# One ordered region from the first stream to the end, with layer 1's first entry laid into turns 10 to 13 of the hyperbolic stage

## The chip, the cores and the metric

The kernel runs on one core of one Trainium2 chip. The metric is the device time of one execution in microseconds (us). Before the change it is 3591.77 us, the median of 3 runs (3590.89 to 3592.56). The core's engines have instruction queues of their own and meet only at semaphores: PE multiplies matrices and transposes tiles, DVE, ACT and POOL work element by element, and SP issues most DMAs.

## The reference

A decoder of two layers works on `x` of 4 sequences of 512 rows and 256 columns, with a context of 4 sequences of 1024 rows and 128 columns. Each block adds to `x`:

```python
x = x + L0_attn(layernorm(x))        # landmark attention
x = x + L0_xattn(layernorm(x), ctx)  # causal attention and attention to the context
x = x + L0_ffn(layernorm(x))         # a linear layer with 6-bit quantisation
x = x + L1_attn(layernorm(x))        # hyperbolic attention, 16 heads of 16
x = x + L1_xattn(layernorm(x), ctx)  # double cross-attention, 16 heads of 32
x = x + L1_ffn(layernorm(x))         # 8 experts, the best 2 of them
```

Two of these matter here. The hyperbolic attention lifts queries and keys onto a hyperboloid, and its scores are the negative squared distances:

```python
neg_inner = einsum('bhie,bhje->bhij', tq, tk) - einsum('bhid,bhjd->bhij', sq, sk)
dist = arccosh(maximum(neg_inner, 1.0 + 1e-07))
scores = -dist ** 2 / sqrt(D)        # then causal mask, softmax, times the spike mask
y = einsum('bhij,bhjd->bhid', attn, v)
```

The double cross-attention, called with an already normalised input, begins with two more norms, the second of them inside its first attention:

```python
x = _ln(xx, ln1_g, ln1_b)            # xx = layernorm(x): a norm of a norm, then scale and shift
xn = _ln(x, lnx_g, lnx_b)            # yn is normed in the same way with lny_g, lny_b
```

## The kernel before, in words

**Stages.** The program runs layer 0's attention, layer 0's cross-attention (a `Stream`, L590 and on, which lays the work of many small attention jobs into steps), layer 1's hyperbolic attention (`l1_attn`, called the hyperbolic stage below), layer 1's cross-attention (`l1_xattn`, another `Stream`) and the experts. Layer 0's quantised linear layer and the lift to the hyperboloid are made in chains of small pieces, one chain for each batch; those that the first stream does not get done are handed on to the hyperbolic stage in a list called `left`.

**Regions.** Inside `with tc.manual_schedule()` instructions keep the order in which the program issues them. Before the change there are three such regions: the first stream's `s.run()`, the loop over the hyperbolic turns, and the second stream's `s.run()` with what follows. What lies outside, and where one region stands against another, is placed by a scheduler. In the built program of before, the first pieces of the second stream stand on DVE's, POOL's and SP's lists in the midst of the hyperbolic turns.

**The hyperbolic stage.** It has 16 units: 4 batches, 2 halves of the heads (`hh`), and 2 pairs of query tiles, (3, 0) and (2, 1). Each pair has 640 columns of causal scores, in 4 tiles `s` (and 4 `mh`) of 128 x 2 x 640. The loop overlaps three units: turn i, in program order on all engines, does

1. for every second turn `fetch`: the DMA of the next `qk` (and `v`) on SP;
2. `squares` of unit i-1: 4 multiplications on POOL (L1047);
3. `roots` of unit i: for each of the 4 tiles two square roots on ACT (L1030, L1031) and an add on POOL (L1032), then two small roots (L1035, L1036) and a small add on POOL (L1037) for the row minima `lm`; then one `pump()`;
4. `scores` of unit i+1: matmuls on PE (L1015, L1019) and clamps on DVE (L1020), which also give the minima;
5. `finish` of unit i-2: transposes, reciprocal and products on DVE; for `hh` = 1 also the projection and the add to `x`;
6. `outputs` of unit i-1: 16 exponentials on ACT (L1066), 10 groups of transposes on PE (L1072), each with a copy on DVE (L1074) and then matmuls (L1059), with a `pump()` after each pair of `gg` and query tile (after copies 4, 5, 9, 10 for the pair (3, 0); 3, 5, 8, 10 for (2, 1));
7. `logs` of unit i: a small logarithm on ACT (L1040), a small square on POOL (L1041), and 4 logarithms on ACT (L1043), which the squares of the next turn need.

The pool of `s` has 9 tiles and that of `mh` has 6. So the second and third roots of turn i need the first five transposes of unit i-2 to be read, and the second half of the scores of unit i+1 waits for POOL's first two adds L1032 of unit i.

**pump.** `left` is a list of chains; each of their items has a gap, counted in calls of `pump`, and a function that issues instructions. One call issues the items of the first chain that are due. Before the change `fetch(b, hh)` pumps until no more than B - 1 - b chains are left, and for the last batch it calls `done()`, which frees the first stream's memory on the right and builds `Early`: the loads of the second stream's first constants and weights (`bc5`, `pv5`, `wk`, `wv`, `wq`).

**The entry.** For each batch of the second stream's first attention, the entry is: a copy of `x` to DRAM (`kept`, DMA on SP); a norm applied twice over (`ln_pieces` with `twice`): two halves of the statistics on DVE (L153 to L159), a power on POOL (L164), `again` (5 small DVE instructions and a second L164), and `apply` in two halves (small DVE instructions L169 to L172 and two L192 each); `enter`, a scale and a shift on POOL (L1141, L1142); and a second norm with one power. In before, `block(k, b)` (L1221 and on) makes all of them and puts them into the second stream's chain.

Of the kernel before, what the change touches and what calls it, by code (L numbers as in the profile page):

```python
# [12 lines left out]
F32 = mybir.dt.float32  # L13
# [7 lines left out]
P = 128  # L21
B, T, C = 4, 512, 256
TC, CC = 1024, 128
NT = T // P
# [13 lines left out]
def decoder_kernel(ctx: ExitStack, tc: tile.TileContext, a: dict, out: bass.AP):  # L38
    nc = tc.nc
    V, G, S, PE = nc.vector, nc.gpsimd, nc.scalar, nc.tensor  # L40

    def ts(i, n=P):
        return slice(i * n, (i + 1) * n)
# [12 lines left out]
    zpool = pool(ctx, "z", 2)  # L56
# [29 lines left out]
    x = const.tile([P, NTILE, C], F32, name="x", tag="x")  # L86
# [430 lines left out]
    def l0_xattn(w, wc, wp, bq, bc2, ct_d, front):  # L517
        with ExitStack() as st:
# [160 lines left out]
            for b in range(B):  # L679
                batch(b)  # L680
            s.chain([(8 + i, 16 + 2 * i, gap, c, f) for i, (gap, c, f) in enumerate(front.weights())])
            with tc.manual_schedule():
                return s.run()

# [252 lines left out]
    def l1_attn(wo, spk, qk_d, v_d, left, done):  # L937
        with ExitStack() as st:
# [27 lines left out]
            units = []  # L966
# [11 lines left out]
            def pump():  # L978
                pump.n += 1
                if left:  # L980
                    c = left[0]
                    while c.items and pump.n >= c.at + c.items[0][2]:
                        c.at = pump.n
                        c.items.popleft()[4]()
                    if not c.items:
                        left.pop(0)
# [3 lines left out]
                c.at = -99  # L990

            def fetch(b, hh):
                while len(left) > B - 1 - b:
                    pump()
                if (b, hh) == (B - 1, 0):
                    done()
                if hh == 0:
                    vs[b] = vp.tile([P, NT, VW], F32, name="v", tag="v")
                    nc.sync.dma_start(vs[b], v_d[b])
                qks[b, hh] = qp.tile([P, 2, 2, T], F32, name="qk", tag="qk")  # L1000
                nc.sync.dma_start(qks[b, hh], qk_d[b][:, :, ts(hh, 2), :])


            def scores(u):
# [21 lines left out]
            def roots(u):  # L1026
                u.s = []
                for m in u.m:
                    s = sp_.tile([P, 2, 640], F32, name="s", tag="s")
                    S.activation(s, m, AF.Sqrt, bias=bpos, scale=2.0**-20)  # L1030
                    S.activation(m, m, AF.Sqrt, bias=bneg, scale=2.0**-20)  # L1031
                    G.tensor_add(s, s, m)  # L1032
                    u.s.append(s)
                u.lm = wk.tile([P, 2, 8], F32, name="lm", tag="lm")
                S.activation(u.lm, u.mn, AF.Sqrt, bias=bpos, scale=2.0**-20)  # L1035
                S.activation(u.mn, u.mn, AF.Sqrt, bias=bneg, scale=2.0**-20)  # L1036
                G.tensor_add(u.lm, u.lm, u.mn)  # L1037

            def logs(u):
                S.activation(u.lm, u.lm, AF.Ln, scale=1024.0)  # L1040
                G.tensor_mul(u.lm, u.lm, u.lm)  # L1041
                for s in u.s:
                    S.activation(s, s, AF.Ln, scale=1024.0)  # L1043

            def squares(u):
                for s in u.s:
                    G.tensor_mul(s, s, s)  # L1047
# [61 lines left out]
                        PE.matmul(ps[:, 0:C], yT[:, c, :], wo[:, c, :], start=c == 0, stop=c == 1)  # L1109
                    add_to(x[:, u.b * NT + qt, :], ps[:, 0:C])  # L1110

            with tc.manual_schedule():
                fetch(0, 0)
                n = len(units)
                prev_o = None
                for i in range(-1, n + 2):
                    u = units[i] if 0 <= i < n else None
                    p = units[i - 1] if 0 <= i - 1 < n else None
                    nx = units[i + 1] if 0 <= i + 1 < n else None
                    if nx and nx.qts[0] == 2 and i >= 0:  # L1120
                        k = 2 * nx.b + nx.hh + 1
                        if k < 2 * B:
                            fetch(k // 2, k % 2)
                    if p:
                        squares(p)
                    if u:
                        roots(u)
                        pump()
                    if nx:
                        scores(nx)  # L1130
                    if prev_o:
                        finish(*prev_o)
                        prev_o = None
                    if p:
                        prev_o = (p, outputs(p))
                    if u:
                        logs(u)


    def affine(dst, src, g, b):  # L1140
        G.tensor_mul(dst, src, mid_bc(g, NT))  # L1141
        G.tensor_add(dst, dst, mid_bc(b, NT))  # L1142


    class Early:
        def __init__(self):
            self.stack = ExitStack()
            self.pl = pool(self.stack, "l5e", 1, "right")
            self.bc5 = load_bc(self.pl, "bc5", 2048)
            self.pv5 = load(self.pl, "pv5", a["pv5"], [P, 44])  # L1150
            self.inner = self.stack.enter_context(ExitStack())
            self.att = pool(self.inner, "l5b", 1, "right")
            self.w = {}
            self.attn_weights("a1", 2, self.w)

        def attn_weights(self, p, nk, w):
            w["k"] = load(self.att, "wk5", rows(f"{p}_wk"), [P, nk, 512])
# [4 lines left out]
    def l1_xattn(cn_d, moe, early):  # L1162
        with early.stack as st:
# [12 lines left out]
            dram = st.enter_context(tc.tile_pool(name="l5x", bufs=1, space=bass.MemoryType.DRAM))  # L1176
            bc5, pv5 = early.bc5, early.pv5
            kept = [dram.tile([P, NT, C], F32, name=f"kept{b}", tag=f"kept{b}") for b in range(B)]
# [42 lines left out]
            def block(k, b):  # L1221
# [5 lines left out]
                e = SimpleNamespace()  # L1227

                def z():
                    if not hasattr(e, "z"):  # L1230
                        e.z = zpool.tile([P, NT, C], F32, name="ln_z", tag="ln_z")
                    return e.z

                def z3():
                    if not hasattr(e, "z3"):
# [2 lines left out]

                def arrive():
                    assert not k or b in back  # L1240

                def enter():
                    affine(x1, e.z, bc5[:, ts(2 * k, C)], bc5[:, ts(2 * k + 1, C)])

                def begin():
                    e.xnT = wk.tile([P, 2, T], F32, name="xnT", tag="xnT")
# [131 lines left out]

                f0, a0 = jobs[k, b, 0].first_d, jobs[k, b, 0].first_a
                own = []  # L1380
                if k == 0:
                    own.append((f0 - 20, f0 - 18, 1, 0.0, lambda: nc.sync.dma_start(kept[b], x1)))
                first, second = ln_pieces(x1, z, twice=k == 0), ln_pieces(x1, z)

                fr = f0 - (12 if k and b == 0 else 20)
                own.append((fr, max(fr, f0 - 17), 0, 0.0, arrive))
# [31 lines left out]
            for k in range(2):  # L1418
                for b in range(B):
                    block(k, b)  # L1420
            with tc.manual_schedule():
                s.run()
                slots.end()

# [382 lines left out]
    with ExitStack() as mid:  # L1807
        mp = pool(mid, "mid", 1)
        dram = mid.enter_context(tc.tile_pool(name="l4d", bufs=1, space=bass.MemoryType.DRAM))
        spk = mp.tile([P, B, NT], F32, name="spk", tag="spk")  # L1810
        qk_d = [dram.tile([P, 2, 4, T], F32, name=f"qk_d{b}", tag=f"qk_d{b}") for b in range(B)]
        v_d = [dram.tile([P, NT, VW], F32, name=f"v_d{b}", tag=f"v_d{b}") for b in range(B)]
        bc3 = load_bc(mp, "bc3", C)
        wqkv = load(mp, "w4", rows("l1_wqkv"), [P, 2, 769], eng=nc.scalar)
        bc4 = load_bc(mp, "bc4", 1026)
        right = mid.enter_context(ExitStack())
        front = Front(right, bc3, wqkv, bc4, spk, qk_d, v_d)
        with ExitStack() as early:
            wp = pool(early, "early", 1)
            first = ExitStack()  # L1820
            fp = pool(first, "first", 1)
            w1 = load(fp, "w1", rows("l0_w"), [P, 2, 768])
            bc1 = load_bc(fp, "bc1", 768)
            w = {n: load(wp, f"w2{n}", rows(f"l0x_{n}"), [P, 2, 512], eng=nc.scalar) for n in ("q", "k", "cq")}
            w["v"] = load(wp, "w2v", rows("l0x_v"), [P, 2, C], eng=nc.scalar)
            wc = {n: load(wp, f"w2{n}", rows(f"l0x_{n}"), [P, 1, m], eng=nc.scalar) for n, m in (("ck", 512), ("cv", C))}
            wo0 = load(wp, "w2p", rows("l0x_p"), [P, 2, C], eng=nc.scalar)
            bq = load(wp, "bq", a["bq"], [P, 16], eng=nc.scalar)
            bc2 = load_bc(wp, "bc2", 768)
            with first as st:  # L1830
                psum_pairs(st)
                l0_attn(w1, bc1)
                context_T(ct_d, cn_d, pvc)
                clear_rows(moe, fp)
            S.preload_act_table_set("natural_log_exp_and_others")
            left = l0_xattn(w, wc, wo0, bq, bc2, ct_d, front)
        mp = pool(mid, "mid2", 1)
        wo1 = load(mp, "w4o", rows("l1_wo"), [P, 2, C])
        early = []

        def done():
            right.close()
            early.append(Early())

        l1_attn(wo1, spk, qk_d, v_d, left, done)
    l1_xattn(cn_d, moe, early[0])

# [83 lines left out]
```

## Time and profile before

| | us |
|---|---|
| median of 3 runs | 3591.77 |
| profiled execution | 3592.31 |
| its span | 3590.6 |
| stretch 0 to 1147: layer 0 | 1147 |
| stretch 1147 to 1710: hyperbolic stage | 563 |
| stretch 1710 to 3200: double cross-attention | 1490 |
| stretch 3200 to 3590: experts | 390 |
| PE, DVE, ACT, POOL busy | 3178.6, 2146.9, 1614.8, 825.2 |

The stretches are cut at round times near the stages' ends. The mean clock that the throttle granted to PE in the profiled execution is 0.918 of full speed. In the stretch from 1540 to 1710 PE is busy for 129.09 of 170.00 us, DVE for 110.22, ACT for 146.67 and POOL for 115.29; from 1710 to 3200 PE is busy for 1418.52 of 1490.

A line of the timeline gives the start in us, the length in us, engine, line of the program, operation, output and inputs with their shapes, how many instructions of a run are put together (x), and in brackets how long the engine had waited before it and for what. L-numbers are lines of the kernel before. In the slices of the page each digit is the busy share of one fortieth of the span, in tenths.

### The profile page before, as it was taken

Reading aid. Unit: us, or ns where it says so; the run is one execution under the profiler, and the core shown is the slowest. Engines: PE = TensorE matmul, PEld = TensorE weight load, DVE = VectorE, ACT = ScalarE, POOL = GpSimd, SP = SyncE. Lnnn points to the kernel's source line nnn. Section 1 sums busy time; section 2 is a strip of 40 time slices with the busy share of each in tenths; the row PEclk is TensorE's granted clock in tenths of the full one; section 3 lists DMA queues with packets and bytes.
Section 4 is the critical chain, followed back from the end, with each engine's and each line's share of the span. In section 5 each row is a group of like instructions: output and inputs, shape, how many; then the busy total and the mean of one; then the engine's idle time right before and its main releaser. Section 6 shows DMA issues by size and latency. Waiting matters only on the chain.

```text
span 3590.6 us, 51432 instructions
## 1 busy us (share of the span) xinstructions
PE 3178.6 (89%) x20119; PEld 1513.5 (42%) x20119; DVE 2146.9 (60%) x5068; ACT 1614.8 (45%) x2860; POOL 825.2 (23%) x763
## 2 busy tenths in 40 slices
PE   6689999999998576687998999999999999989994
PEld 3433333334334343444333344433333333448994
DVE  4576666776775778766666555555646656443112
ACT  2235554454554876697233334334443343433331
POOL 1010112122022845676122121110101111020003
PEclk9789999999998576788899999999999999989997
DMA  8200000000002000300000000000000000035885
GB/s 274 66 14 7 1 7 4 24 10 7 24 1 70 24 1 31 107 13 7 24 1 1 1 1 18 7 1 30 13 1 13 7 1 15 4 110 206 317 328 170
DMA packets 81396, 176.13 MB, mean 49 GB/s; under 512 B 6265, under 2 KB 63745, under 8 KB 76033
## 3 DMA queue, kind: packets, MB, share of 16 engines
q1 hardware_dynamic: 76016, 161.16, 12.7%
q0 software_dynamic: 3072, 8.39, 0.8%
q8 instruction: 158, 2.59, 0.3%
q10 hardware_dynamic: 2064, 3.29, 0.3%
q14 instruction: 86, 0.70, 0.1%
HBM read 127.48 MB, written 45.34 MB: 48 GB/s over the span
## 4 chain that ended last, share of the span: by engine, by line
PE 69%; DVE 16%; ACT 4%; issue 4%; DMA 3%; POOL 2%; SPq 0%; POOLq 0%; ACTq 0%; DVEq 0%
PE ps_s L363 16%; PE ps_g L452 7%; PE ps_s L389 5%; PE ps_g L459 4%; PE ps_s L1742 3%; PE ps_s L1749 3%; PE ps_s L1342 3%; PE ps_s L1282 3%; PE ps_s L588 3%; DVE mx L371 3%; PE ps_s L1327 3%; PE ps_s L382 3%; PE ps_s L1072 2%; PE ps_s L1314 1%; DMA rows<-ln_z,idx 1%
## 5 line engine op out<-in xcount | busy, mean ns | idle before, releaser
L390 ACT ACTIVATE pt<-ps_s 128x512 f32<-128x512 f32 (+2 forms) x1536 | 791.4, 569 | 1033.5 <-PE ps_s L389 895.5
L371 DVE TENSOR_REDUCE mx<-ps_s 128x1 f32<-128x512 f32 x1280 | 818.5, 684 | 415.5 <-PE ps_s L363 307.6
L363 PE MATMUL ps_s<-kT,qT 32*128 32x512 f32 (+3 forms) x3072 | 921.7, 623 | 41.6 <-DVE mx L371 39.5
L389 PE MATMUL ps_s<-qa,kT 32*128 32x512 f32 (+3 forms) x1536 | 446.7, 599 | 3.0 <-DVE mx L371 1.6
L363 PEld LDWEIGHTS ps_s<-kT,qT 32*128 32x128 f32 x3072 | 307.1, 186 | 322.0 <-DVE mx L371 133.7
L389 PE MATMUL ps_s<-qT,kT 32*128 32x512 f32 x1536 | 410.5, 624 | 0.0
L459 PE MATMUL ps_g<-pt,onesf 128*32 128x512 f32 x1536 | 214.0, 629 | 0.0
L1032 POOL TENSOR_TENSOR s<-s,mh 128x1280 f32<-128x1280 f32 x64 | 186.9, 2945 | 68.0 <-ACT mh L1031 49.1
L164 POOL TENSOR_TENSOR ln_r<-ln_ve,mhalf 128x4 f32<-128x4 f32 x40 | 41.1, 1028 | 625.7 <-DVE ln_ve L159 560.9
L1303 POOL TENSOR_TENSOR yT<-o 128x128 f32<-128x128 f32 x128 | 58.1, 457 | 535.1 <-DVE o L1302 532.8
L1744 ACT ACTIVATE hid<-ps_s,we 128x128 f32<-128x128 f32 x312 | 89.0, 370 | 201.4 <-PE ps_s L1742 163.0
L367 DVE CUSTOM_DVE_ANT_0 junk<-ps_s,dmask 128x512 f32<-128x512 f32 (+3 forms) x256 | 125.7, 491 | 88.2 <-PE ps_s L363 44.9
L389 PEld LDWEIGHTS ps_s<-qa,kT 32*128 32x128 f32 x1536 | 148.7, 188 | 52.0 <-DVE mx L371 31.1
L1015 PE MATMUL ps_s<-qk 32*128 32x256 f32 (+3 forms) x512 | 103.1, 609 | 62.9 <-DVE mh L1020 56.6
L382 PE MATMUL ps_s<-qm,all 3*128 3x512 bf16 x768 | 149.3, 387 | 6.5 <-DVE v L1290 4.0
L1742 PE MATMUL ps_s<-zsT,we 128*128 128x128 f32 x1248 | 148.1, 277 | 7.8 <-DVE zsT L1733 7.3
L1742 PEld LDWEIGHTS ps_s<-zsT,we 128*128 128x128 f32 x1248 | 146.4, 194 | 11.8 <-DVE zsT L1733 8.6
L1047 POOL TENSOR_TENSOR s<-s 128x1280 f32<-128x1280 f32 x64 | 147.6, 2339 | 12.3 <-ACT s L1043 12.3
L1072 PE MATMUL ps_s<-ident,s 128*128 128x128 f32 x640 | 129.7, 340 | 18.3 <-ACT s L1066 17.1
L1074 DVE COPY pt<-ps_s 128x512 f32<-128x512 f32 x160 | 108.6, 688 | 56.7 <-PE ps_s L1072 56.5
L1749 PE MATMUL ps_s<-we,hid 128*128 128x256 f32 x624 | 141.0, 379 | 0.0
L452 PE MATMUL ps_g<-pt,vc 128*32 128x512 f32 x1024 | 138.2, 611 | 0.0
(425 smaller groups left out, 4986.7 us busy)
## 6 DMA issues: line engine op xcount, KB each, us to landing
we<-in_we SPq DMA_DIRECT2D x39, 2052.0 KB, 10.0
rows<-zero SPq DMA_DIRECT2D x8, 2048.0 KB, 16.7
qk_d<-qkT SPq DMA_DIRECT2D x32, 256.0 KB, 2.6
qk<-qk_d SPq DMA_DIRECT2D x8, 1024.0 KB, 6.5
zs<-rows SPq DMA_DIRECT2D x39, 128.0 KB, 4.8
outs<-ys SPq DMA_DIRECT2D x39, 128.0 KB, 5.3
li<-in_a_li SPq DMA_DIRECT2D x4, 1024.0 KB, 8.7
v_d<-vp SPq DMA_DIRECT2D x16, 143.5 KB, 1.8
```

The lines of the kernel that those rows point to most:

```text
L363: PE.matmul(ps[:, 0:n], u.qT[r, ts(qt)], u.kT[r, hf * 512 : hf * 512 + n], start=True, stop=True)
L371: V.tensor_reduce(m, ps[:, 0:n], AX.X, ALU.max)
L382: PE.matmul(ps, self.ones[r, :], u.qm[r, :], start=True, stop=False)
L389: PE.matmul(ps[:, c0:], u.kT[r, ts(kt)], (u.qa if u.first_row else u.qT)[r, c0:], start=u.first_row, stop=True)
L390: S.activation(u.pt[:, j, c0:], ps[:, c0:], AF.Exp, scale=u.scale)
L452: PE.matmul(o[r, c0:], u.v(kt, j), pt[:, j, c0:], start=first, stop=last)
L459: PE.matmul(acc[ts(j, 32), 1, :], self.onesf, pt[:, j, :], start=i == 0, stop=i == u.nkt - 1)
L1032: G.tensor_add(s, s, m)
L1047: G.tensor_mul(s, s, s)
L1072: PE.transpose(ps[:, ts(j)], u.s[h // 2][:, h % 2, c0 : c0 + P], ident)
L1742: PE.matmul(ps[:, ts(f)], u.w[:, k : k + P], u.zT[:, c, :], start=c == 0, stop=c == 1)
L1749: PE.matmul(ps[:, 0:C], u.h[:, f, :], u.w[:, 2048 + f * C : 2048 + f * C + C], start=f == 0, stop=f == 7)
```

## The change

Two things are done. First, one region takes the place of the three: it is opened before the first stream's table of activations is loaded and closed at the end of the second stream, so that everything in between keeps the order in which the program issues it. Second, the entry of batch 0 is no longer built by `block(0, 0)`. A new method `Early.entry` makes the pieces of an entry, and `Early.pieces` puts those of the first one, with the copy `kept[0]`, into one chain, which `done()` appends to `left`; so `pump` issues them in the hyperbolic turns. `fetch` pumps only when `hh` is 0, and calls `done()` behind the loads of `v` and `qk`; after the loop the rest of `left` is pumped. The `kept` tiles are made in `Early`.

With the gaps given, the pieces fall so in program order: in turn 10 the copy `kept[0]` (after the roots), the two halves of the statistics (after copies 3 and 5 of the outputs) and `again` (after copy 10); in turn 11 the two halves of `apply` (after copies 4 and 9) and `enter` (after copy 10); in turn 12 the second norm's statistics and its first `apply` half (after copy 10); in turn 13 the second half. PE's and ACT's lists are the same as before. On POOL, the two powers stand between L1037 and L1041 of turn 10, the affine L1141 and L1142 there in turn 11, the power of the second norm there in turn 12. On SP, `v` and `qk` of batch 3 stand before the loads of `bc5`, `pv5`, `wk`, `wv`, `wq`; `kept[0]` after them; then `qk` of batch 3's other half, `li1`, `li2`, `li3` and `kept` of batches 1 to 3.

```diff
@@ l0_xattn
-            with tc.manual_schedule():
-                return s.run()
+            return s.run()
@@ l1_attn
             def fetch(b, hh):
-                while len(left) > B - 1 - b:
+                while hh == 0 and len(left) > B - 1 - b:
                     pump()
-                if (b, hh) == (B - 1, 0):
-                    done()
                 if hh == 0:
                     vs[b] = vp.tile([P, NT, VW], F32, name="v", tag="v")
                     nc.sync.dma_start(vs[b], v_d[b])
                 qks[b, hh] = qp.tile([P, 2, 2, T], F32, name="qk", tag="qk")
                 nc.sync.dma_start(qks[b, hh], qk_d[b][:, :, ts(hh, 2), :])
+                if (b, hh) == (B - 1, 0):
+                    done()
...
-            with tc.manual_schedule():
-                fetch(0, 0)
-                n = len(units)
...
+            fetch(0, 0)
+            n = len(units)
...
+            while left:
+                pump()
@@ class Early, __init__
+            dram = self.stack.enter_context(tc.tile_pool(name="l5x", bufs=1, space=bass.MemoryType.DRAM))
+            self.kept = [dram.tile([P, NT, C], F32, name=f"kept{b}", tag=f"kept{b}") for b in range(B)]
+            self.e = SimpleNamespace()
+
+        def entry(self, k, b, e):
+            x1 = x[:, ts(b, NT), :]
+            def z():
+                if not hasattr(e, "z"):
+                    e.z = zpool.tile([P, NT, C], F32, name="ln_z", tag="ln_z")
+                return e.z
+            def enter():
+                affine(x1, e.z, self.bc5[:, ts(2 * k, C)], self.bc5[:, ts(2 * k + 1, C)])
+            return ln_pieces(x1, z, twice=k == 0), enter, ln_pieces(x1, z)
+
+        def pieces(self):
+            first, enter, second = self.entry(0, 0, self.e)
+            work = [(1, 0.0, lambda: nc.sync.dma_start(self.kept[0], x[:, 0:NT, :]))]
+            work += [(2 if i > 1 else 1, 0.0, p) for i, p in enumerate(first)] + [(1, 0.0, enter)]
+            return work + [(2 if i in (0, 2) else 1, 0.0, p) for i, p in enumerate(second)]
@@ l1_xattn, block(k, b)
+                begun = (k, b) == (0, 0)
+                e = early.e if begun else SimpleNamespace()
...
-                if k == 0:
+                if k == 0 and not begun:
                     own.append((f0 - 20, f0 - 18, 1, 0.0, lambda: nc.sync.dma_start(kept[b], x1)))
-                first, second = ln_pieces(x1, z, twice=k == 0), ln_pieces(x1, z)
+                first, enter, second = ([], lambda: None, []) if begun else early.entry(k, b, e)
...
-            with tc.manual_schedule():
-                s.run()
-                slots.end()
+            s.run()
+            slots.end()
@@ the program
+            ordered = ExitStack()
+            ordered.enter_context(tc.manual_schedule())
             S.preload_act_table_set("natural_log_exp_and_others")
             left = l0_xattn(w, wc, wo0, bq, bc2, ct_d, front)
...
         def done():
             right.close()
             early.append(Early())
+            work = early[0].pieces()
+            left.append(SimpleNamespace(items=deque((0, 0, gap, c, f) for gap, c, f in work), at=-99))
...
     l1_xattn(cn_d, moe, early[0])
+    ordered.close()
```

More of the change, by code (lines that the diff above doesn't have):

```diff
@@ L1110, in finish @@
                     add_to(x[:, u.b * NT + qt, :], ps[:, 0:C])
-            with tc.manual_schedule():
-                fetch(0, 0)
-                n = len(units)
[L1115 to L1137, printed above, removed]
+            fetch(0, 0)
+            n = len(units)
+            prev_o = None
+            for i in range(-1, n + 2):
+                u = units[i] if 0 <= i < n else None
+                p = units[i - 1] if 0 <= i - 1 < n else None
+                nx = units[i + 1] if 0 <= i + 1 < n else None
+                if nx and nx.qts[0] == 2 and i >= 0:
+                    k = 2 * nx.b + nx.hh + 1
+                    if k < 2 * B:
+                        fetch(k // 2, k % 2)
+                if p:
+                    squares(p)
+                if u:
+                    roots(u)
+                    pump()
+                if nx:
+                    scores(nx)
+                if prev_o:
+                    finish(*prev_o)
+                    prev_o = None
+                if p:
+                    prev_o = (p, outputs(p))
+                if u:
+                    logs(u)
+            while left:
+                pump()
     def affine(dst, src, g, b):
@@ L1175, in l1_xattn @@
             ptp = pool(inner, "l5p", 2)
-            dram = st.enter_context(tc.tile_pool(name="l5x", bufs=1, space=bass.MemoryType.DRAM))
             bc5, pv5 = early.bc5, early.pv5
-            kept = [dram.tile([P, NT, C], F32, name=f"kept{b}", tag=f"kept{b}") for b in range(B)]
+            kept = early.kept
             onesf = att.tile([P, 32], F32, name="onesf", tag="onesf")
@@ L1226, in block @@
                 bl1, bl3 = bc5[:, ts(4 + 2 * k, C)], bc5[:, ts(5 + 2 * k, C)]
[L1227 to L1232, printed above, removed]
+                begun = (k, b) == (0, 0)
+                e = early.e if begun else SimpleNamespace()
                 def z3():
@@ L1240, in arrive @@
                     assert not k or b in back
-                def enter():
-                    affine(x1, e.z, bc5[:, ts(2 * k, C)], bc5[:, ts(2 * k + 1, C)])
                 def begin():
```

## The prediction

> **What bounds the kernel now.** First the page's slices (89.8 us each): PE is the full row everywhere except slices 14 to 19, the hyperbolic stage, where ACT rises.
>
> ```profile
> span 3590.6 us, 51432 instructions
> PE   6689999999998576687998999999999999989994
> ACT  2235554454554876697233334334443343433331
> ```
>
> Then the timeline of each engine there. A plain turn (here turn 11):
>
> ```profile
> 1563.22 7.36 ACT L1066 ACTIVATE s<-s,lm 128x512 f32<-128x512 f32 x16
> 1570.48 0.20 ACT L1040 ACTIVATE lm<-lm 128x16 f32<-128x16 f32 x1
> 1576.63 1.36 ACT L1030 ACTIVATE s<-mh,bpos 128x1280 f32<-128x1280 f32 x1
> ...
> 1566.51 0.21 POOL L1037 TENSOR_TENSOR lm<-lm,mn 128x16 f32<-128x16 f32 x1
> 1570.75 0.22 POOL L1041 TENSOR_TENSOR lm<-lm 128x16 f32<-128x16 f32 x1 [4.03 <-ACT lm L1040]
> 1571.91 9.16 POOL L1047 TENSOR_TENSOR s<-s 128x1280 f32<-128x1280 f32 x4 [0.94 <-ACT s L1043]
> 1581.03 11.46 POOL L1032 TENSOR_TENSOR s<-s,mh 128x1280 f32<-128x1280 f32 x4
> ```
>
> Call the start of the exponentials (L1066) in turn i E_i: E9 1495.95, E10 1537.26, E11 1563.22, then 25.96 apart up to E15 1667.06. ACT has no gap in 25.96, so a plain turn is ACT's. POOL works 21 of the 26 and rests only between L1037 and L1041. L1037 ends at E+3.5, and ACT's L1040 needs it at E+7.26: POOL may be 3.8 us late, no more. Next, what happens when something is late:
>
> ```profile
> 1500.59 2.35 POOL L1141 TENSOR_TENSOR x<-ln_z,bc 128x1024 f32<-128x1024 f32 x1 [3.28 <-DMA bc<-in_bc]
> ...
> 1505.40 0.43 DVE L155 BATCH_NORM_STATS2 ln_st<-x 128x6 f32<-128x256 f32 x1 [2.82 <-POOL x L1142]
> 1509.56 2.28 DVE L169 TENSOR_TENSOR ln_t<-ln_r 128x4 f32<-128x4 f32 x1 [1.13 <-POOL ln_r L164]
> 1516.43 2.24 DVE L172 TENSOR_TENSOR ln_r<-ln_r,ln_t 128x4 f32<-128x4 f32 x1
> 1518.70 3.25 DVE L192 TENSOR_SCALAR ln_z<-x,ln_mv,ln_r 128x256 f32<-128x256 f32 x2
> 1522.54 1.27 DVE L1074 COPY pt<-ps_s 128x512 f32<-128x512 f32 x2
> ...
> 1527.35 1.36 ACT L1030 ACTIVATE s<-mh,bpos 128x1280 f32<-128x1280 f32 x1 [15.24 <-DVE pt L1074]
> ```
>
> That is turn 9: the entry of layer 1 holds the copies L1074, and ACT stands 15.24 us. Four single waits complete the picture:
>
> ```profile
> 1351.13 0.22 ACT L1040 ACTIVATE lm<-lm 128x16 f32<-128x16 f32 x1 [9.04 <-POOL lm L1037]
> ...
> 1375.49 0.66 PE L1059 MATMUL ps_g<-pt,v 128*32 128x128 f32 x8 [5.99 <-DVE pt L1074]
> ...
> 1380.68 0.16 DVE L172 TENSOR_TENSOR ln_r<-ln_r,ln_t 128x4 f32<-128x4 f32 x1
> ...
> 1583.96 0.56 DVE L1020 TENSOR_SCALAR_CACHE_REDUCE mh<-ps_s 128x384 f32<-128x384 f32 x1 [1.68 <-POOL s L1032]
> ```
>
> A late POOL stops ACT at L1040; late DVE stops PE; L172 costs 0.16 with POOL idle but 2.24 while POOL runs; and the second half of the scores (L1020) waits for POOL's first two adds L1032.
>
> **What the change removes.** In before the entry's first norm sits in turns 5 and 6, its affine and second norm in turn 9.
>
> Turn 9 without it: the scores end at 1502.33; finish with its projection takes 7.9 (1618.32 to 1626.20 in turn 13), so the copies start at 1510.2 instead of 1522.54. ACT's second root needs the fifth transposes, 4.44 after the first copy (1626.20 to 1630.64): 1514.75 instead of 1527.35. Turn 9 lasts 28.7, not 41.3: −12.65. Ends: −8.0 (only the DMA wait and the two affines) and −15.3 (down to a plain turn).
>
> Turn 6: DVE's entry work between 1359 and 1389 leads to PE's 5.99 above and a smaller one. Without it the second token's L826 starts at 1367.0 (after L842) instead of 1373.04, but its L828 then meets POOL's L1032 (1366.95 to 1369.9), and the fourth token's L828 the add after ACT's late roots. Followed to the output copy at 1389.47, that leaves −4.4. Ends: −1.1 (POOL's power, 1.13, alone) and −9.3 (all of PE's waits there: 5.99, 0.68, 1.60, 1.07).
>
> **What it adds.** PE and ACT keep their order in the built program. POOL's is now: two powers (L164) between L1037 and L1041 of turn 10, the affine (L1141, L1142) there in turn 11, one power there in turn 12. Each waits for DVE pieces that lie inside the outputs, and L1041, the squares L1047 and the adds L1032 queue behind. Unlocked prices: a half of the statistics 1.07, `again` 1.4, `apply` 1.75 and 0.75, a power 1.02, the affine 4.75. Times go on from E10 = 1524.65, leaving turn 6 aside.
>
> Turn 10: the copies start at 1529.8; statistics end at 1535.9; `again` follows the tenth copy (1540.65) and ends at 1542.05; the second power ends at 1543.1. L1047 starts at 1543.4, where a plain turn has E+8.69 = 1533.3: 10.1 late. L1037 of turn 11 ends at 1564.2 (9.1 + 11.5 later), L1040 wanted it at 1557.9. ACT stands 6.35.
>
> Turn 11: the second half of the scores waits for the adds at 1555.4 and 1558.3; finish meets two adds; copies start at 1564.4, `apply` ends at 1575.1, the affine at 1579.9. L1047 1580.15, L1037 of turn 12 at 1600.9. ACT wanted it at 1590.2: 10.7, and two of its roots then wait 2.4 and 1.0 for late transposes.
>
> Turn 12: scores again wait for adds (1592.15, 1595.0), finish meets two more and projects; copies start at 1607.7, the power is done at 1615.5. POOL now catches up without a rest to 1636.5, and `apply` (from 1619.15) meets it: L169 to L172 and L192 take 12.2, as the same ones took 12.3 in turn 9 of before. Then scores to 1642.0, finish with locks, copies at 1651.75.
>
> Turn 13: ACT waits 6.1 at L1040 and 10.85 for the transposes (1656.2). E14 = 1666.1, E15 = 1692.05, and from there ACT leads as before.
>
> So E11 to E12 is 32.35 (+6.4), to E13 40.1 (+14.1), to E14 43.05 (+17.1): +37.6. Lower end: copies always at E+3.1 and no locks: L1047 at least 6.6 late in turn 10 and 10 in turn 11, less 3.8 each: +9. Upper: the second L192 of each pair locked too, twice 2.87: +43.3. I take 37.6, as each link has its row above.
>
> The Trainium skill (SBUF — State Buffer, "Who interferes with whom") says that of a VectorE instruction in a two-port mode, or with two SBUF inputs, and a GpSimd one, the later blocks until the other is through. Rows 2.24 and 0.16 agree. It speaks against laying small VectorE steps beside a busy POOL, and taken for each instruction it would lock both L192 of a pair, the upper end: 3618. The row 3.25 for two shows one lock, but POOL rested after it.
>
> **At nothing.** v and qk of batch 3 now go ahead of bc5 on SP (0.34 + 0.53 us): bc5 is read some 70 us later. The kept copy of batch 0 lands 2.6 us after issue, long before turn 11; without that cover it would hold the affine. li1 moves behind qk: first read at 1889. li3 now stands before the kept copies of batches 1 to 3, waits until 1704 as before, so batch 1's lands near 1707.6; its affine runs at 1732.05. That cover gone, POOL would wait there. The memsets and identb only swap places.
>
> **Sum.** −12.65 − 4.4 + 37.6 = +20.6. The profiled execution took 3592.31 (span 3590.6 and 1.7 around), 0.54 over the median 3591.77 of three runs; on that median: 3612.3.
>
> **Rivals.** Faster: POOL's holds stay inside its 3.8 us, only −17.1 is left: 3574.7. It decides at turn 10's L1047: before 1537 it is hidden. Against it: the power must wait for the tenth copy, E+13 at the soonest. Chance 0.08. Milder: the holds as worked out, but POOL is through when `apply` comes in turn 12, so 10.85 goes: 3601.4; for it speaks that E13 could shift by a few us, against it that POOL is 14 us behind. 0.17. Harsher: both L192 locked, 3618 and up with the next scores late: 0.12. No effect: the two norms cost the same wherever they lie, 3592; against it, 15.24 goes from one wait and returns on POOL: 0.05. The forecast: 0.58.
>
> **Numbers.** A run tells 0.2% (7.2 us) from no change. Faster 0.08, same 0.05 (no effect), slower 0.87 (forecast, milder, harsher). The range 3594 to 3627 leaves out the faster case and the ends of the others.
>
> **What would show it.** Right: turn 9 near 29 us; POOL idle before L164 in turn 10 and before L1141 in turn 11 for DVE; ACT waiting at L1040 for L1037 in three turns, 6 to 11 each; L169 to L172 over 2 us each in turn 12. Wrong: L1040 never waits, or turns 10 to 13 stay at 26.

## The result

The changed kernel takes 3612.81 us, the median of 5 runs (3610.21 to 3614.08); the kernel before takes 3591.77 (5 runs, 3587.57 to 3592.56). The ratio is 1.006, with a 95% interval of 1.0045 to 1.0074: slower by 21 us. The forecast was 3612. The profiled execution took 3611.71 us, 19.4 more than that of before, with a span of 3610.0.

The page's slices of the changed kernel (90.3 us each):

```profile
span 3610.0 us, 51409 instructions
PE   6689999999998576856898999999999999989994
ACT  2235554454554776777233343344344343433331
```

PE's row has a new dip behind the place where the entry was laid (5 and 6 instead of 8 and 7, about 1625 to 1805). Instructions of the hyperbolic stage have line numbers lower by one than before (L1040 is L1039, L1037 is L1036, L1047 is L1046, L1066 is L1065). The time between the first exponentials of successive turns, taken from ACT's timeline, tells turn by turn where the time went (a plain turn is 25.96):

| us | turn 9 | 10 | 11 | 12 | 13 | 14 | 10 to 14 over plain |
|---|---|---|---|---|---|---|---|
| before | 41.31 | 25.96 | 25.96 | 25.96 | 25.96 | 25.96 | 0 |
| changed | 28.33 | 25.96 | 31.81 | 39.11 | 47.69 | 25.96 | 40.7 |

The waits of ACT in these turns, from its timeline:

```profile
1514.19 1.36 ACT L1029 ACTIVATE s<-mh,bpos 128x1280 f32<-128x1280 f32 x1 [2.26 <-DVE pt L1073]
1563.09 0.21 ACT L1039 ACTIVATE lm<-lm 128x16 f32<-128x16 f32 x1 [5.68 <-POOL lm L1036]
...
1600.25 0.22 ACT L1039 ACTIVATE lm<-lm 128x16 f32<-128x16 f32 x1 [8.83 <-POOL lm L1036]
...
1635.13 0.22 ACT L1039 ACTIVATE lm<-lm 128x16 f32<-128x16 f32 x1 [6.80 <-POOL lm L1036]
1658.76 1.36 ACT L1029 ACTIVATE s<-mh,bpos 128x1280 f32<-128x1280 f32 x1 [14.70 <-DVE pt L1073]
```

The 15.24 of turn 9 is 2.26. In its place the small logarithm waits for POOL three times, and in turn 13 the roots wait 14.70 for the copies. POOL's timeline shows why it is late: its entry pieces stand in front of its own work and wait for DVE.

```profile
1535.64 1.02 POOL L164 TENSOR_TENSOR ln_r<-ln_ve,mhalf 128x4 f32<-128x4 f32 x1 [9.74 <-DVE ln_ve L159]
1541.18 1.01 POOL L164 TENSOR_TENSOR ln_r<-ln_v,mhalf 128x4 f32<-128x4 f32 x1 [4.52 <-DVE ln_v L179]
...
1574.59 2.36 POOL L1141 TENSOR_TENSOR x<-ln_z,bc 128x1024 f32<-128x1024 f32 x1 [11.54 <-DVE ln_z L192]
...
1613.09 1.02 POOL L164 TENSOR_TENSOR ln_r<-ln_ve,mhalf 128x4 f32<-128x4 f32 x1 [12.88 <-DVE ln_ve L159]
```

And DVE's timeline shows what fills the end of turn 12, once POOL runs without a rest:

```profile
1617.20 1.67 DVE L169 TENSOR_TENSOR ln_t<-ln_r 128x4 f32<-128x4 f32 x1
1618.91 2.24 DVE L170 TENSOR_TENSOR ln_t<-ln_t,ln_ve 128x4 f32<-128x4 f32 x1
1621.18 2.25 DVE L171 TENSOR_SCALAR ln_t<-ln_t 128x4 f32<-128x4 f32 x1
1623.47 2.81 DVE L172 TENSOR_TENSOR ln_r<-ln_r,ln_t 128x4 f32<-128x4 f32 x1
1626.31 5.83 DVE L192 TENSOR_SCALAR ln_z<-x,ln_mv,ln_r 128x256 f32<-128x256 f32 x2
1632.66 2.69 DVE L192 TENSOR_SCALAR ln_z<-x,ln_mv,ln_r 128x256 f32<-128x256 f32 x2
```

POOL works there from 1614.26 to 1635.10 without a rest. At the first exponentials of turn 15 (1694.63 against 1667.06) the changed kernel is 27.6 us late, at the end 19.4. So 8.2 came back in the second stream, where nothing was changed for it.

### The profile page after: what moved, and what is told of

It is laid out like the page before. It is cut to its first block, busy times and chain, and to the rows that moved or that the text cites. A ratio compares the mean times of both kernels' runs of the same rounds, so it can differ in the third digit from the quotient of the medians.

```text
span 3610.0 us, 51409 instructions
## 1 busy us (share of the span) xinstructions
PE 3168.9 (88%) x20119; PEld 1512.8 (42%) x20119; DVE 2155.4 (60%) x5068; ACT 1615.0 (45%) x2860; POOL 823.9 (23%) x763
## 3 DMA queue, kind: packets, MB, share of 16 engines
q8 instruction: 158, 2.59, 0.3%
## 4 chain that ended last, share of the span: by engine, by line
PE 69%; DVE 16%; issue 4%; ACT 4%; DMA 3%; POOL 3%; SPq 0%; POOLq 0%; DVEq 0%; ACTq 0%
PE ps_s L363 16%; PE ps_g L452 7%; PE ps_s L389 5%; PE ps_g L459 4%; PE ps_s L1757 4%; PE ps_s L1764 4%; PE ps_s L1358 3%; PE ps_s L1298 3%; PE ps_s L588 3%; DVE mx L371 3%; PE ps_s L1343 3%; PE ps_s L382 3%; PE ps_s L1071 2%; PE ps_s L1330 1%; DMA rows<-ln_z,idx 1%
## 5 line engine op out<-in xcount | busy, mean ns | idle before, releaser
L164 POOL TENSOR_TENSOR ln_r<-ln_ve,mhalf 128x4 f32<-128x4 f32 x40 | 41.1, 1026 | 642.1 <-DVE ln_ve L159 577.5
L1046 POOL TENSOR_TENSOR s<-s 128x1280 f32<-128x1280 f32 x64 | 147.6, 2337 | 10.4 <-ACT s L1042 10.4
L1019 DVE TENSOR_SCALAR_CACHE_REDUCE mh<-ps_s 128x512 f32<-128x512 f32 (+3 forms) x256 | 108.6, 487 | 66.4 <-POOL s L1031 44.7
```

## The experiments

The theory: the time is lost because POOL, which takes its instructions in order, is held by entry pieces whose DVE inputs come late, and because DVE's small steps are locked while POOL runs. The rivals: the ordered region costs something by itself; or the entry's work, 10.7 us of DVE and 7.8 of POOL, costs by its size wherever it is laid in these turns.

All times below are medians, against runs of the kernel before on the same chip. Executions of one kernel differ by 10 us and more there, so the turns, read from the one profiled execution of each kernel, are the sharper measure. The kernel before took 3590.61 us beside the first four rows, 3591.53 beside the next three and the first split, which ran on another chip, and 3591.40 beside the last two, on the first of the two chips again:

| us | turn 9 | 10 | 11 | 12 | 13 | 14 | 10 to 14 over plain | time | ratio to before (95%) |
|---|---|---|---|---|---|---|---|---|---|
| no work | 28.33 | 25.96 | 25.97 | 25.96 | 25.97 | 25.96 | 0.0 | 3580.43 | 0.997 (0.996 to 0.998) |
| POOL ready | 28.53 | 25.97 | 33.47 | 34.22 | 36.34 | 25.96 | 26.2 | 3602.54 | 1.0032 (1.002 to 1.0043) |
| wait only | 35.64 | 25.97 | 30.79 | 34.26 | 33.65 | 25.96 | 20.8 | 3594.45 | 1.0009 (1.0 to 1.0018) |
| no second norm | 28.33 | 25.96 | 31.79 | 38.50 | 26.90 | 25.96 | 19.3 | 3595.99 | 1.0015 (1.0004 to 1.0027) |
| region only | 28.33 | 25.96 | 25.97 | 25.96 | 25.96 | 25.96 | 0.0 | 3596.97 | 1.0021 (1.0009 to 1.0032) |
| move only | 28.32 | 25.96 | 31.78 | 39.10 | 47.70 | 25.96 | 40.7 | 3616.55 | 1.0072 (1.0057 to 1.0088) |
| changed, again | 28.39 | 25.96 | 31.80 | 39.11 | 47.69 | 25.96 | 40.7 | 3619.73 | 1.0081 (1.0061 to 1.0101) |
| split | 35.66 | 25.97 | 25.97 | 25.95 | 29.30 | 25.96 | 3.4 | 3582.16 | 0.9967 (0.9953 to 0.9981) |
| split, again | 28.37 | 25.97 | 25.96 | 25.97 | 25.97 | 25.96 | 0.0 | 3577.86 | 0.9956 (0.9942 to 0.9971) |
| split, affine later | 35.66 | 25.96 | 25.96 | 25.96 | 25.96 | 25.97 | 0.0 | 3578.97 | 0.9966 (0.9955 to 0.9978) |

### The entry's work left out

```diff
...
-            work += [(2 if i > 1 else 1, 0.0, p) for i, p in enumerate(first)] + [(1, 0.0, enter)]
-            return work + [(2 if i in (0, 2) else 1, 0.0, p) for i, p in enumerate(second)]
...
+                nc.sync.dma_start(self.e.z, x[:, 0:NT, :])
...
```

> The changed kernel without the entry's arithmetic: no statistics, powers, affine or norm products for batch 0 of layer 1; its tile is filled by one DMA from x, so that part of the computation is left out. Theory (the entry's pieces held POOL, and DVE's small ones were locked): the 40.7 us that turns 11 to 13 took over plain ones vanish, turns 10 to 14 take 25.96 each, and the time is 3612.8 - 40.7 = 3572. Rival (the single ordered region costs something by itself): turns 10 to 14 stay above 28 or a stage elsewhere is longer, and the time is 3590 or more. The run also gives the floor for all that follows.

Turns 10 to 14 are plain, so the region costs them nothing, and the entry's pieces account for all of the 40.7. The time is 8 above the 3572 expected. That figure took 40.7 off a time that already held the 8.2 given back after the stage; this kernel's lag in the profile hardly changes there (-17.3 at turn 15, -15.7 at the end), and without the 8.2 the sum is 3580.3.

### POOL's pieces made ready

```diff
-            G.tensor_tensor(r, ve, mhalf, ALU.pow)
+            G.tensor_tensor(r, ve if ready is None else ready, mhalf, ALU.pow)
...
-                affine(x1, e.z, self.bc5[:, ts(2 * k, C)], self.bc5[:, ts(2 * k + 1, C)])
+                affine(self.spare, bc, self.bc5[:, ts(0, C)], self.bc5[:, ts(1, C)])
```

> The changed kernel with POOL's five entry instructions in the same places and of the same size, but reading tiles that are ready long before (a tile of ones, the constants), the affine writing a spare tile: POOL waits for no piece of DVE, the output is not the norm's. DVE's work is the same. Rival (only POOL's waiting costs): turns 11 to 13 go back to 26 or 27 each, 3575 to 3580. Theory with locks (what was POOL's wait becomes DVE's lock, since again, after copy 10, and apply, after copy 4, now meet POOL's squares): again's seven small steps take some 2.2 each, 15 instead of 1.4, apply's five likewise 10 instead of 1, less 3.5 per turn that the scores have to spare: 3595 to 3615.

The theory with locks holds, at 26.2 over plain turns. ACT never waits at the small logarithm now; it waits for PE's and DVE's part of the outputs:

```profile
1573.04 1.36 ACT L1029 ACTIVATE s<-mh,bpos 128x1280 f32<-128x1280 f32 x1 [7.26 <-PE ps_s L1071]
1606.78 1.36 ACT L1029 ACTIVATE s<-mh,bpos 128x1280 f32<-128x1280 f32 x1 [7.54 <-PE ps_s L1071]
...
1643.74 1.36 ACT L1029 ACTIVATE s<-mh,bpos 128x1280 f32<-128x1280 f32 x1 [10.28 <-DVE pt L1073]
```

DVE's timeline of this kernel, behind copy 10 of turn 10, and under it POOL's four adds that run meanwhile:

```profile
1541.55 2.82 DVE L170 TENSOR_TENSOR ln_t<-ln_t,ln_ve 128x4 f32<-128x4 f32 x1
1544.40 2.82 DVE L171 TENSOR_SCALAR ln_t<-ln_t 128x4 f32<-128x4 f32 x1
1547.26 2.80 DVE L172 TENSOR_TENSOR ln_r<-ln_r,ln_t 128x4 f32<-128x4 f32 x1
1550.10 2.81 DVE L177 TENSOR_TENSOR ln_v<-ln_r 128x4 f32<-128x4 f32 x1
```

```profile
1541.45 11.44 POOL L1031 TENSOR_TENSOR s<-s,mh 128x1280 f32<-128x1280 f32 x4
```

In the changed kernel the same steps took 0.15 to 0.17 each, since there POOL stood waiting for them. DVE's timeline of the changed kernel, the same two steps:

```profile
1539.94 0.16 DVE L170 TENSOR_TENSOR ln_t<-ln_t,ln_ve 128x4 f32<-128x4 f32 x1
1540.14 0.17 DVE L171 TENSOR_SCALAR ln_t<-ln_t 128x4 f32<-128x4 f32 x1
```

So `again` takes 13.9 us instead of 1.1: with POOL's wait gone, DVE's steps are locked instead. Not every lock that was expected came. The five steps of `apply` in turn 11 took 0.15 to 0.17, as POOL happened to wait for transposes there (5.57); in that turn the lock fell on the second pair of L192 (3.50). Two changes were made at once here, readiness and a spare target; together they add one memset of 0.10 us on POOL, in turn 9.

### The waits alone

```diff
...
+            def tiny():
...
+                V.tensor_scalar_add(self.ve, one, 1e-5)
...
+            work = [(1, 0.0, move), (1, 0.0, tiny), (1, 0.0, both), (2, 0.0, both)]
+            work += [(2, 0.0, tiny), (2, 0.0, tiny), (1, 0.0, power)]
+            return work + [(2, 0.0, tiny), (1, 0.0, both), (2, 0.0, tiny), (1, 0.0, tiny)]
```

> The changed kernel with each piece cut to one small DVE instruction and each POOL piece to one power of 128 x 4 on its result, in the same places (the affine one power too); the norm itself is left out and its tile filled by a DMA. Theory (the wait in POOL's order is what costs, not the work): the second power of turn 10 still waits for copy 10, L1047 there is 6.6 late instead of 10, and the holds of turns 11 and 12 stay: turns 11 to 13 together 16 to 20 over plain ones, 3588 to 3592. Rival (the entry's bulk on DVE and POOL costs): 3572 to 3576, no wait at the small logarithm for POOL.

With nine small instructions on DVE and four powers on POOL in the entry's place, half of the loss stays: 20.8 over plain turns, where the theory had 16 to 20 and the rival nothing. ACT's timeline has the same three waits:

```profile
1572.46 0.22 ACT L1039 ACTIVATE lm<-lm 128x16 f32<-128x16 f32 x1 [4.73 <-POOL lm L1036]
1605.22 0.21 ACT L1039 ACTIVATE lm<-lm 128x16 f32<-128x16 f32 x1 [6.69 <-POOL lm L1036]
...
1638.51 0.21 ACT L1039 ACTIVATE lm<-lm 128x16 f32<-128x16 f32 x1 [5.72 <-POOL lm L1036]
```

The work is next to nothing, and the place in POOL's order is enough. How much it costs is less sure than that it does: the profiled execution, 3610.27, was the slowest of 11, and by the medians this kernel is only 14.0 over the one without the work. The time, 3594.45, is 2.5 above the range expected. (Turn 9 at 35.64 is taken up below.)

### Without the second norm

```diff
-            return work + [(2 if i in (0, 2) else 1, 0.0, p) for i, p in enumerate(second)]
+            return work
```

> The changed kernel without the second norm in turns 12 and 13 (left out; the flip reads the first norm's tile). Theory: turn 11 stays at 31.8 and turn 12 near 37.5, as both follow from the pieces of turns 10 and 11; turn 13 falls from 47.7 to 26 or 27, since neither the power holds POOL nor the locked steps hold the transposes: 3612.8 - 21.7 - 1.5 = 3589.6, 3587 to 3593. Rival (each piece costs by its size; the second norm has 5.4 of the entry's 18.5 us on DVE and POOL): 12 of the 40.7 go, 3601.

Turns 11 and 12 stay (31.79, 38.50) and turn 13 falls to 26.90: 21.4 of the 40.7 hang on one power and seventeen DVE instructions that were laid where POOL is busy. By size they would have had 12. The time, 3595.99, is 3 above the range expected; again the sum had the 8.2 in it, of which this kernel gives back 4.0 (7.3 late at turn 15, 3.3 at the end).

### The region alone, and the move alone

The first leaves the chain to `block(0, 0)`:

```diff
-            work = early[0].pieces()
-            left.append(SimpleNamespace(items=deque((0, 0, gap, c, f) for gap, c, f in work), at=-99))
...
-                begun = (k, b) == (0, 0)
+                begun = False
```

> The one ordered region, but the entry of batch 0 built by its block again, so at the start of the second stream. Theory: the hyperbolic turns go as without the entry (turns 10 to 14 at 25.96), and the entry's chain then stands in the open before the first flip: statistics 2.1, power 1.0, again 1.4, power 1.0, apply 2.5, affine 4.7, statistics 2.1, power 1.0, apply 2.3 and some 2 of handovers, 20 over 3580.4: 3598 to 3602. Rival (the second stream has other work to cover it, the region alone is the gain): 3580 to 3584.

The turns are plain, and between turn 15 and the first flip of the second stream the lag against before goes from -13.0 to +7.2: the entry in the open costs 20.3, or 18.4 more than the same stretch of the kernel without the entry's work (65.2 against 46.8 us). PE's timeline at that flip:

```profile
1717.77 2.21 PE L1272 MATMUL ps_s<-ident,ln_z 128*128 128x128 f32 x8 [18.69 <-DVE ln_z L192]
```

In before the entry sat in turns 5, 6 and 9, at a price of 13 in turn 9 and 1 to 5 in turn 5. So the region alone takes from the entry the place that the scheduler had found for it. The time, 3596.97, is 1 below the range expected.

The second restores the three regions around the changed entry:

```diff
-            return s.run()
+            with tc.manual_schedule():
+                return s.run()
...
```

> The entry laid into turns 10 to 13 as in the changed kernel, but with the three regions of before instead of one. Theory (the region has no part in the loss; PE's, ACT's and DVE's order and POOL's entry pieces stay): turns 11 to 13 take 31.8, 39.1 and 47.7 again, 3608 to 3616. Rival (the region keeps something from being placed better): near 3592, and other turns than these.

The turns are those of the changed kernel to 0.03; the time, 3616.55, is 0.6 above the range expected. The loss is the placing's, not the region's.

### The entry split

Each piece is cut in its DVE and its POOL part, and a table of places takes the place of the chain:

```diff
...
+                (10, "copy", 3): [lambda: a.stats(0)],
+                (10, "copy", 5): [lambda: a.stats(1)],
+                (11, "roots"): [a.power],
+                (11, "copy", 2): [a.again, a.power2],
+                (12, "project", 0): [lambda: a.apply(0)],
+                (12, "project", 1): [lambda: a.apply(1)],
+                (13, "roots"): [mul, add],
+                (14, "copy", 3): [lambda: b.stats(0)],
+                (14, "copy", 5): [lambda: b.stats(1)],
+                (15, "roots"): [b.power],
+                (15, "copy", 2): [lambda: b.apply(0)],
+                (15, "copy", 3): [lambda: b.apply(1)],
...
```

"roots" is the place behind the small add L1036, "copy" behind a copy of the outputs, "project" ahead of an add of the projection.

> The same entry, whole, laid so that POOL's pieces never stand ahead of unready DVE work and DVE's small steps run while POOL rests: each power one turn after its statistics, directly behind the small add of the minima; again after copy 2 of turn 11; the first apply beside the two projection matmuls of turn 12, the affine behind the small add of turn 13, the second statistics in turn 14, its power and apply in turn 15. Theory: no wait of the small logarithm for POOL, no lock over 2 us in the entry, turns 10 to 14 between 25.96 and 27.5 each, so 0 to 5 over the kernel without the entry's work (3580.4 on this chip): 3580 to 3585. Rival (the entry's 18.5 us of DVE and POOL cost by their size wherever they lie in these turns): 3592 to 3599, no better than the kernel before.

The same work, whole, now costs 3.4 over plain turns, and the kernel beats the one before by 9 us. (The 3580.4 was measured on the other chip, not on this one; the kernel before differs by 0.9 between the two.) The small steps of `apply` took 1.7 to 2.8 for the second norm in turn 12 of the changed kernel. Here they take 0.15 to 0.17 for either norm: in turn 12 POOL rests for 3.81 us, between its small add and its small square. DVE's timeline, turn 12 of the split kernel (the second profiled execution of it; L224 is the L172 of before, L241 the L187, L246 the scaling L192, L265 the add to `x`):

```profile
1578.62 0.16 DVE L224 TENSOR_TENSOR ln_r<-ln_r,ln_t 128x4 f32<-128x4 f32 x1
1578.82 0.16 DVE L241 TENSOR_TENSOR ln_r<-ln_r 128x4 f32<-128x4 f32 x1
1579.02 0.73 DVE L246 TENSOR_SCALAR ln_z<-x,ln_mv,ln_r 128x256 f32<-128x256 f32 x2
1580.29 0.42 DVE L265 TENSOR_TENSOR x<-ps_s,x 128x256 f32<-128x256 f32 x1 [0.54 <-PE ps_s L1168]
```

They fill the wait of 2.17 that DVE has there for the projection in a plain turn; 0.54 is left of it. Behind the turns of the table nothing is added either: from turn 15 to the end the lag against before goes from -15.3 to -13.5, and without the entry's work from -17.3 to -15.7.

Turn 13 at 29.30, above the 27.5 expected, was put down to the affine, which met the products of the finish (2.04 and 2.18 us). So it was moved by a turn:

```diff
-                (13, "roots"): [mul, add],
-                (14, "copy", 3): [lambda: b.stats(0)],
-                (14, "copy", 5): [lambda: b.stats(1)],
+                (14, "roots"): [mul, add],
+                (14, "copy", 8): [lambda: b.stats(0)],
+                (14, "copy", 10): [lambda: b.stats(1)],
```

> The split entry with one step moved: the affine stands behind the small add of turn 14 instead of turn 13, the second statistics after copies 8 and 10 of turn 14. In the split kernel turn 13 took 29.30, since the affine met the reciprocal products of turn 13's finish (2.04 and 2.18 us each) ahead of a projection. Theory (in turn 14, which has no projection, the affine meets only copies): turns 10 to 14 all between 25.96 and 26.5, 3 us less than the split kernel beside it, some 10 to 14 under the kernel before. Rival (the affine locks something in turn 14 as well): turn 13 falls to 26 and turn 14 rises by as much, the same time as the split kernel.

> The split kernel once more on the same chip, as the measure for the one with the affine later. Its turns 10 to 14 should repeat (25.97, 25.97, 25.95, 29.30, 25.96). Turn 9 took 35.66 in its first profile, where 12.3 us of clock were withheld in the turn before against 5 to 7 in most other profiles: if that is the throttle and not the kernel, turn 9 shows 28.3 here as in the others; if it belongs to the kernel, 35.7 again. Time 8 to 11 us under the kernel before.

All turns are plain with the affine later, as the theory had it. But the split kernel's own turn 13 is 25.97 in its second profiled execution, on the other chip, so the reading of 29.30 was too simple. There only one of the two products was locked (2.07; the other took 0.23). Of the two profiles the affine costs something only in the one in which turn 9 had run late; two are too few to say that this is the condition. Turn 9 took 35.66 in one execution of the split kernel and 28.37 in the other. The windows from the exponentials of turn 8 to those of turn 9 (after the busy times of the engines come the granted clock, the DMA share and GB/s), first execution, then second:

```profile
1458.16:1493.00 34.84, 25.58 (x181) 15.95 (x178) 25.89 (x57) 25.95 (x33) 21.10 (x11) 0.65 0.15 46
```

```profile
1459.34:1493.59 34.25, 27.26 (x212) 17.09 (x209) 25.30 (x63) 25.95 (x33) 21.44 (x11) 0.80 0.18 56
```

A granted clock of 0.65 in that window goes with a turn 9 of 35.6 in all three profiles that have it (split, wait only, affine later), 0.80 or 0.85 with 28.3 to 28.5 in the eight others without the entry there. Both kinds were met on both chips. The version with the affine later had the late turn 9 in its profile and still no loss behind it. Between the version with the affine later and the split beside it, 3578.97 and 3577.86, the runs can't decide. Both beat the kernel before, by 12 to 14 us.

### What came back after the stage

> The changed kernel once more, beside the others on this chip. What is open: of the 27.6 us by which it was late at the last exponentials, 8.2 were back by the end, 4 of them where the projection's matmuls ran at 1.13 us instead of 2.08 under a higher granted clock. If that belongs to the kernel, the start of the second stream shows 1.13 again and the lag shrinks by 6 to 10 after turn 15; if it is the throttle's phase in one execution, it shrinks by another amount, anywhere from -4 to 10, and the time lies within 3605 to 3620.

In the second profiled execution the lag goes from 23.5 at turn 15 to 19.5 at the end: 4.0 back, not 8.2. So the matmuls show 1.13 again, as the first case asked, but the lag shrinks by less than its 6 to 10. These 4.0 are the same in both profiles of the changed kernel, at the last projection and the first features of the second stream. PE's timeline of before and, under it, of the changed kernel:

```profile
1708.20 2.08 PE L1109 MATMUL ps_s<-w4o,yT 128*128 128x256 f32 x4 [0.52 <-DVE yT L1106]
```

```profile
1734.99 1.13 PE L1108 MATMUL ps_s<-w4o,yT 128*128 128x256 f32 x4 [0.63 <-DVE yT L1105]
```

The granted clock was 0.50 in the window 1705 to 1710 of before and 1.00 in 1730 to 1735 of the changed kernel. The move alone, which has the same turns, shows 2.08 there and gives back 1.6 in all (20.8 late at turn 15, 19.2 at the end). So the turns don't settle it; whether the changed kernel reaches this place in a better phase of the clock by rule or by chance stays open. The other 4.2 of the first profile came near 3050 to 3120, and the second profile doesn't have them.

## Why the prediction was right

The time, its direction and the mechanism were right; that the sum came out so near was partly luck, because errors cancelled. In the later runs the changed kernel's median is 28.2 over before (3619.73 against 3591.53), not 21.0. By its own steps, with the two profiles of the changed kernel:

- **Turn 9, -12.65.** Measured -12.98 and -12.92 (41.31 to 28.33 and 28.39), and -12.8 to -13.0 in all profiles without the late turn 9. Right.
- **Turn 6, -4.4, between -1.1 and -9.3.** The wait lies between the first exponentials of turns 5 and 6. It went from 54.45 to 53.47 and 50.11: -0.98, just outside the ends given, and -4.34. The prediction had said that the lift's own steps meet POOL's adds once the entry's are gone; which of them do differs between the two executions. DVE's timeline of the changed kernel, first execution:

```profile
1363.70 1.67 DVE L827 TENSOR_TENSOR q_t<-qk 128x512 f32<-128x512 f32 x1
...
1366.97 2.96 DVE L841 TENSOR_TENSOR mk<-mk,q_t 128x32 f32<-128x32 f32 x1
...
1370.56 2.68 DVE L827 TENSOR_TENSOR q_t<-qk 128x512 f32<-128x512 f32 x1
...
1385.05 3.12 DVE L827 TENSOR_TENSOR q_t<-qk 128x512 f32<-128x512 f32 x1
```

  In the second execution L841 took 0.21. In before the entry's own steps took these locks at 2.53, 1.31, 2.84 and 2.83.
- **Turn 10's hold.** L1047 was to start at 1543.4 after E10 at 1524.65, so 18.75 behind; it started at 1542.33 after 1524.10, 18.2 behind. Turn 11: +6.4 forecast, +5.85 measured.
- **Turn 11's affine.** ACT was to stand 10.7 at the small logarithm and 2.4 and 1.0 for transposes; it stood 8.83, 1.27 and 0.51, and 1.16 and 0.83 between its exponentials for POOL's squares. Turn 12: +14.1 forecast, +13.15 measured.
- **Turn 12's locks.** Here a term was mis-sized. The steps from L169 to the first pair of L192 were put at 12.2, as in turn 9 of before, where that pair took 3.25 because POOL rested after it, and the second pair was counted at its unlocked 0.75. Measured: 1617.20 to 1632.1, 14.9, with 5.83 for the first pair, and 2.69 for the second. That is 4.6 more, and turn 13 went to +21.73 instead of +17.1. That these two differences agree so well is in part chance: the finish behind them took 11.5 instead of the 9.75 counted, with its products locked at 1.72 and 2.59, and the scores and the way from the first copy to the root took less than counted. The harsher rival had priced the lock of both L192; its chance of 0.12 was too low, for POOL had 20 us of late work before it. The Trainium skill (SBUF — State Buffer, "Who interferes with whom"), taken for each instruction as the prediction weighed it, comes nearer here than the row that the prediction took: both L192 of the first pair show the lock.
- **Behind the stage, nothing.** The sum was carried to the end unchanged. Measured: -8.2 and -4.0, with the clock.
- **The signs.** Turn 9 is near 29, POOL is idle before L164 and L1141, and ACT waits at the small logarithm in three turns. Two sizes fall short of what was named: the first of these waits is 5.68, not 6, and L169 in turn 12 is 1.67, not 2.
- **At nothing.** POOL's affine waited for DVE's L192, not for `bc5` or `kept`; and the next batch's, in the second stream, waited 6.05 for L192 as before, not for its copy. Right.

So the sum of +20.6 stands against -0.2 up to turn 9, -13.0 in it, +40.7 and -8.2, which makes +19.4, and in the second profile against -4.3, -12.9, +40.7 and -4.0, +19.5. The faster rival asked for holds inside 3.8 us; they were 9 and more. The milder one asked for POOL to be through when the second norm's `apply` comes, and it was not. The rival of no effect is refuted by the split: the same two norms cost from 0 to 41 us in turns 10 to 14 by their place.

## What to carry to other kernels

Before work is laid into the idle time of an in-order engine, look at when its inputs are ready there: a small instruction that waits holds all that is queued behind it, and the engine's slack (3.8 us here) is spent at once. Give each engine's part of a piece a place of its own, the consumer's a stage later than the producer's, where it finds its input ready. And lay small VectorE steps where GpSimd rests: in the chains of this case a locked step cost up to one whole instruction of the other engine (2.8 us for 128 x 4 elements, 2.9 for 128 x 256).

## What the runs showed of the hardware

A locked DVE step ended with the POOL instruction that ran beside it: 2.80 to 2.82 us for 128 x 4 elements in the run with POOL ready, where POOL's adds took 2.9 each, against 0.16 alone. The statistics (0.42 and 0.39 us) and the copies from PSUM (0.69) kept their length beside a running POOL; an add of a constant to 128 x 4 elements in SBUF (L159) didn't, at 2.03 instead of 0.17.

Executions of one kernel on one chip lay far apart: 3608.66 to 3633.59 for the changed kernel, 3570.77 to 3580.55 for the split one. In the profiles the plain turns, led by ACT, repeat to 0.01 us, while turn 9 differs by 7.3 with the granted clock of the stretch before it. The Trainium skill (TensorE: Matmul & The Clock Gate, "What's actually happening") says that the clock is granted by a window that runs freely, not in step with the kernel, so that the point of change differs between runs. That agrees with the two executions of the split kernel, but no run here shows the window itself.
